# Two residual convolution layers on one core: statistics loads three chunks ahead, the next image's weights on GpSimd, and a reordered handover between the layers

## The chip, the cores and the metric

The kernel runs on one core of a Trainium2 chip. The metric is the device time of one execution in microseconds (us). It is given as the median of several executions, and one further execution was recorded by the profiler; the views quoted below come from that one.

## The reference, cut to what matters

The input `x` has four images of 64 channels and 256 x 256 pixels, in fp32. Two layers follow each other, and each adds its result to its input.

```python
# layer 0, on the group-normalized input
h  = gelu(conv3x3(gn(x), c1_w) + c1_b)
xa, k = split(conv1x1(h, c2_w), 2)
xs = gelu(conv_vertical3(conv_horizontal3(xa)))          # depthwise
w  = softmax(mean(xs) @ gate_w.T); keep the two largest of three
out = xs + sum_i w_i * w3_i @ ((w2_i @ k) * (w1_i @ xs))  # three low-rank experts
x = x + conv1x1(out, proj_w)
# layer 1, on the group-normalized result
h = relu(batchnorm(conv3x3(gn(x), quantized(w1))))        # statistics over all four images
h = batchnorm(conv3x3(h, quantized(w2)))                  # the same
x = x + relu(h + gn(x))
```

Both group norms need the mean and variance of a whole image before that image can be used, and both batch norms need those of all four images before anything behind them can start.

## The kernel before, in words

**Tiling.** The 128 partitions hold 64 channels of two image rows; an image has 128 such row pairs. A chunk is 8 row pairs (16 chunks an image, 1 MiB each), a group is 2, an octet is 4 (32 octets an image).

**Stages.** (1) The statistics of image 0 (`stats_load`, `stats_group`, `stats_end`, L370 to L416). (2) Layer 0 for four images, a software-pipelined loop of 32 steps an image, one octet a step. The 3x3 convolution is done as products over pixel pairs: GpSimd forms four sums and differences of neighbouring pixels in `v_ring` (`front_v`, L479), TensorE multiplies them with `c1s` and `u12` (`front_conv_a` and `_b`, through the helper at L436), ScalarE and VectorE undo the pair transform (`front_butterfly`, L545 to L547), ScalarE applies gelu (`front_h`, L553). Two and three steps later come the taps (`front_taps_a`, `_b`, `_h`, L602 to L620), the projection (`front_proj`, whose add on VectorE is L651), and the low-rank products (`front_k` L627, `front_q` L664 with L668 on VectorE). In the same loop, one image behind, `out_octets` adds the experts' part (L737 to L748), and one image ahead the next image's statistics are taken: `stats_load` issues one chunk on SyncE, `stats_group` is one `bn_stats` on VectorE (L383), and `stats_end` makes mean, scale and from these the next image's weights `c1s`, `u12` and the zero-point tile `v_edge` (L397 to L411). (3) `conv1`, the first convolution of layer 1, 32 blocks an image. Each chunk of the normalized image is split for it into an upper part (ScalarE, L343) and a lower part (the remainder; first cut of five rows on VectorE, second on GpSimd, L345), and so are sums of pixel pairs (GpSimd L353 and L361, ScalarE L359). A block is 16 products into `ps_h` and 4 into `ps_hm` (both L301), then ScalarE forms `m` (L324) and VectorE `h` (L325) and the batch statistics (L827). (4) `conv2` in the same manner. (5) The end: transfers, one ScalarE pass and two VectorE passes a chunk.

**What sets the order.** Everything from stage 2 on is written into a plan: `at(step, order, call)`, and within a step calls are issued by their order number. Each engine runs its own instructions in that order, and SyncE issues nearly all DMAs in that order too, so an instruction that waits holds up all behind it on its engine. In a step of layer 0 the orders that matter are: image loads 0, first products 1, outputs 2, statistics groups 3.5, taps 4, `divide` 5, projection 6, second products 7, butterfly 7.5, gelu 8.5, `front_v` 9 and 9.5, ps_k and ps_q 10, taps' exit 11, statistics load 11.5. The steps of conv1 use orders from 12 on. `divide` (L429) is a small memset on GpSimd (`tick`): it waits for the taps' last product, and the second products wait for it.

**The buffers concerned.** PSUM has two buffers of tag `c` (`ps_c`, `ps_h`), one of tag `a` (`ps_a`, `ps_hm`) and one of tag `p` (`ps_k`, `ps_p`, `ps_q`, `ps_o` and the small products of the statistics). SBUF tiles of tag `half` in `first_pool` hold statistics chunks (places called "s", two of them) and later the first pair of conv1's halves; work tiles "o" (three) hold statistics chunks of images 0 and 1 and later the outputs' chunks.

**The statistics' places and distance.** Images 0 and 1 use the places s, s, o, o, o in turn; images 2 and 3 the two s alone. In the plan, chunk k of image 1 is loaded three chunks ahead of its use, and chunks of images 2 and 3 one chunk ahead; 2.7 groups are taken a step:

```python
before, tags = (3, STATS_IN) if b == 1 else (1, STATS_IN[:2])
at(t + int((k - before) * CG / per), 11.5, stats_load, b, k, *tags[k % len(tags)])
```

**The handover.** Steps are counted on: image b begins at step 32 b, and `CONV1` is 128. The last image's steps from 128 on are spread out, three conv1 steps to one of layer 0 (`tail`, L873), so that octets 29 to 31 finish between conv1's first blocks. Of conv1's first image, chunks 0 to 3 have places of their own in the plan (`plan_conv1`), with the pixel-pair sums of a chunk made right after its split (`conv1_add_sums`).

Of the kernel before, what the change touches and what calls it, by code (L numbers as in the profile page):

```python
# [9 lines left out]
F32 = mybir.dt.float32  # L10
F32R = mybir.dt.float32r
# [51 lines left out]
def conv_preact_kernel(ctx: ExitStack, tc: tile.TileContext, io, col128, colset, col64):  # L63
# [51 lines left out]
    def half_pads(tiles):  # L115

        for t in tiles:
            nc.gpsimd.memset(t.bitcast(F32)[:, :, HW : HW + 1], 0.0)
        return tiles
# [2 lines left out]

        return t[:, a:e, :].rearrange("p a (e j) -> p a e j", e=2)[:, :, :, 0:HW]

    def sum_tiles(pool, name):
        return [pool.tile([P, CPAIR + 1, HW], F32R, tag="sum", name=f"sum_{name}{j}", bufs=4) for j in range(2)]

    def chunk_x(name):
        return first_pool.tile([P, CPAIR, PW], F32, tag="x", name=name, bufs=1)

    def split_tiles(pool, name):

        return [half_pads([half_tile(pool, f"half_{name}{i}{j}", 4) for j in range(2)]) for i in range(2)]


    lstat = layers.enter_context(tc.tile_pool(name="lstat", bufs=2))
# [196 lines left out]

    CUTS = (0, 5), (5, CPAIR + 1)

    def split(tiles, y, engines):

        parts = []
        for a, e in CUTS:
            upper, lower = (by_pixels(t, a, e) for t in tiles)  # L340
            parts.append((upper, lower, y[:, a:e, :].rearrange("p a (j e) -> p a e j", e=2)))
        for upper, _, y in parts:
            nc.scalar.activation(upper, y, AF.Copy)  # L343
        for (upper, lower, y), engine in zip(parts, engines):
            engine.tensor_tensor(lower, y, upper.bitcast(F32), ALU.subtract)  # L345
# [23 lines left out]

    def stats_load(b, k, tag, bufs):  # L370
        if tag == "s":
            t = flat(half_tile(first_pool, f"xs_in_{b}_{k}", 2, F32))[:, 0 : CPAIR * W]
            x_in[b, k] = t.rearrange("p (a b) -> p a b", b=W)
        else:
            x_in[b, k] = chunk_out(f"xs_in_{b}_{k}", tag, bufs)
        nc.sync.dma_start(flat(x_in[b, k]), x_s[b][:, k * CPAIR * W : (k + 1) * CPAIR * W])
# [8 lines left out]
    def stats_end(b):  # L385


        own = stat.tile([P, 2], F32, tag="gx", name=f"gx_{b}")
        yield from group_norm(st_x.pop(b), c128("avgx"), own, f"x{b}")
        yield  # L390
        gn1[b] = stat.tile([P, 2], F32, tag="gn1", name=f"gn1_{b}")
        v_edge[b] = lstat.tile([P, W // 2], F32, tag="v_edge", name=f"v_edge_{b}")
        ps = small(f"ps_gx_{b}")
        nc.tensor.matmul(ps[:, 0:2], c128("from_x"), own, start=True, stop=True)
        nc.vector.tensor_copy(gn1[b], ps[:, 0:2])
        c1s[b] = lstat.tile([P, 3, 3, C], F32, tag="c1s", name=f"c1s_{b}")
        nc.vector.tensor_scalar(  # L397
            c1s[b].rearrange("p a b c -> p (a b c)"), c128("c1"), gn1[b][:, 1:2], None, ALU.mult
        )
        nc.vector.tensor_scalar(v_edge[b], zeros[:, 0 : W // 2], gn1[b][:, 0:1], 2.0, ALU.add, ALU.mult)  # L400
        u12[b] = lstat.tile([P, 3, 2, C], F32, tag="u12", name=f"u12_{b}")
        ends = lstat.tile([P, 3, C], F32, tag="u_ends", name=f"u_ends_{b}", bufs=1)
        nc.vector.tensor_tensor(ends, c1s[b][:, :, 0, :], c1s[b][:, :, 2, :], ALU.add)
        for i, op in enumerate((ALU.add, ALU.subtract)):
            nc.vector.tensor_tensor(u12[b][:, :, i, :], ends, c1s[b][:, :, 1, :], op)

        nc.vector.tensor_tensor(ends[:, 0, :], u12[b][:, 0, 0, :], u12[b][:, 1, 0, :], ALU.add)
        for half in (slice(0, C), slice(C, P)):
            nc.vector.tensor_tensor(both[half, half], ends[half, 0, :], u12[b][half, 2, 0, :], ALU.add)
        u = u12[b].rearrange("p a b c -> p (a b c)")  # L410
        nc.vector.tensor_scalar(u, u, 0.5, None, ALU.mult)  # L411
# [394 lines left out]
    def conv1_b(b, d):  # L806
        k, i = d // 2, d % 2 * 2 * GP
        st = st_h[b]
        ps, ps_m = open_h.pop(b), bank("a", f"ps_hm_{b}_{d}")
        convolve_even(ps, "w1", halves[k % 2], i, 2 * GP)  # L810
        convolve_sum(ps_m, "w1", sums[k % 2], i, 2 * GP)
        if i == 0:

            if k % 2 and (b > 0 or k > 2):
                h_out[b] = chunk_x(f"h1_{b}_{k}").rearrange("p a b -> p (a b)")[:, 0 : CPAIR * W]
                h_out[b] = h_out[b].rearrange("p (a b) -> p a b", b=W)
            else:
# [25 lines left out]


    weights()
    STATS_IN = ("s", 2), ("s", 2), ("o", 3), ("o", 3), ("o", 3)
    for k in range(NCH):
        stats_load(0, k, *STATS_IN[k % 5])
        for g in range(k * CG, (k + 1) * CG):
            stats_group(0, g)  # L850
    for k in range(2):
# [20 lines left out]

    def tail(step):  # L873

        return step if step < CONV1 else CONV1 + 3 * (step - CONV1)

    def plan_front(b):
        t = b * F_STEPS
# [26 lines left out]
            at(place(t + 2 * j + 4), 10, front_k, b, j)  # L905
            at(place(t + 2 * j + 5), 10, front_q, b, j)
        e = place(t + NOCT + 3)
        at_each(((e, 2.5), (e, 5.7), (e, 8.7)) if e < CONV1 else ((e, 2.5), (e + 2, 12.7), (e + 4, 12.7)), gate(b))

    def plan_stats(b, t, per):  # L910

        for k in range(NCH):

            before, tags = (3, STATS_IN) if b == 1 else (1, STATS_IN[:2])
            at(t + int((k - before) * CG / per), 11.5, stats_load, b, k, *tags[k % len(tags)])
        for g in range(NG):
# [13 lines left out]

    conv1_pool, halves, sums = [], [], []

    def conv1_open():

        front.close()
        pool = layers.enter_context(tc.tile_pool(name="conv1", bufs=2, reuse_waits="tile"))
        conv1_pool.append(pool)
        halves.append(half_pads([half_tile(pool, f"half_11{j}", 2) for j in range(2)]))
        sums.extend(sum_tiles(pool, f"1{i}") for i in range(2))

    def plan_conv1(b):
# [75 lines left out]
        if k == NCH - 1:  # L1017
            nc.gpsimd.memset(h[0:C, CPAIR, :], 0.0)

    def conv2_split(i):  # L1020
        split(halves2[i % 2], h_in[i], (nc.vector, nc.vector))

    def conv2_add(i):
        sums_in[i] = add_pixels(h_in[i], f"2_{i}", halves_pool, "s", 2, [P, 5 * HW])
# [15 lines left out]
    sums2 = [sum_tiles(halves_pool, f"2{i}") for i in range(2)]  # L1040
    h2, st_h2 = {}, {}

    def chunk_h2(b, k):
# [27 lines left out]
    with tc.manual_schedule(  # L1071
# [179 lines left out]
```

## Time and profile before

| | |
|---|---|
| Median of 3 executions | 3432.7 us (3428.28 to 3432.73) |
| Profiled execution: its own time | 3435.02 us |
| Its span in the profile | 3433.2 us |
| Busy: TensorE, VectorE, ScalarE, GpSimd | 2753.0, 2723.4, 1673.7, 1593.8 us |
| 16 DMA engines | 838.28 MB, 73.3% of the span |
| Granted TensorE clock, mean | 0.91 |

The page shows the span in 40 equal slices, a digit for the busy tenths of each. Idle time of an engine costs nothing by itself; it costs where the engine is the one that all others wait for. So the views to read are those of waits: each line has who waited, for whom, how long in total, how often, and the longest. The timeline of one engine lists its instructions with start and length, and in brackets the idle time ahead of one and what ended it. In a plan like this one a wait is often put down to the neighbour in the queue and not to its cause: the instruction that the neighbour stands behind has to be looked up on its engine.

### The profile page before, as it was taken

To read this page: it belongs to the slowest core of one execution; us is meant where nothing else is said; L and a number is where in the kernel's file an instruction comes from. 1 tells how busy PE (TensorE), PEld (TensorE's weight loads), DVE (VectorE), ACT (ScalarE), POOL (GpSimd) and SP (SyncE) were. 2 spreads that over 40 slices of the span, in tenths; PEclk is the share of its full clock that TensorE was granted. 3 is DMA by queue.
4 is the path that set the end of the run, shared out by engine and by line. 5 is a ranking of instruction groups with operands and counts; after the bars stand their busy time and mean duration, and the time that the engine had idled before them with its cause. 6 is when DMAs were issued, how large, how long until landed. Compare 5 with 4: busy or idle time off the path is not lost.

```text
span 3433.2 us, 60883 instructions
## 1 busy us (share of the span) xinstructions
PE 2753.0 (80%) x24832; PEld 1764.3 (51%) x24832; DVE 2723.4 (79%) x2997; ACT 1673.7 (49%) x1831; POOL 1593.8 (46%) x1806
## 2 busy tenths in 40 slices
PE   2999999999999999996799999998999999400000
PEld 1555544454444545553577776786877777300000
DVE  7676578877878777774699999898999999856665
ACT  0444433343333344334466666676777777422222
POOL 2444433333333344443487878675777777200000
PEclk9999999999999999998899999999999999755555
DMA  8665578877887666774587888574666665599999
GB/s 301 171 186 119 149 220 256 242 207 223 236 257 229 202 190 203 217 208 140 174 286 271 304 283 285 205 261 167 239 235 240 235 232 183 177 412 413 412 412 384
DMA packets 365671, 838.28 MB, mean 244 GB/s; under 512 B 23312, under 2 KB 285968, under 8 KB 302672
## 3 DMA queue, kind: packets, MB, share of 16 engines
q1 hardware_dynamic: 365392, 834.40, 73.3%
q8 instruction: 195, 3.19, 0.4%
q14 instruction: 84, 0.69, 0.1%
HBM read 493.00 MB, written 341.31 MB: 243 GB/s over the span
## 4 chain that ended last, share of the span: by engine, by line
PE 70%; DMA 12%; DVE 10%; SPq 2%; ACT 2%; issue 2%; POOL 1%; ACTq 0%; DVEq 0%; POOLq 0%
PE ps_h L301 25%; PE ps_c L436 18%; DMA y_end<-y_d 9%; PE ps_a L436 8%; PE ps_k L627 4%; PE ps_h2m L301 3%; PE ps_o L737 3%; PE ps_p L436 3%; PE ps_hm L301 3%; PE ps_q L664 2%; DMA xs_in<-in_x 2%; DVE half L345 1%; DVE st_x L383 1%; DVE h L325 1%; SPq L1138 1%
## 5 line engine op out<-in xcount | busy, mean ns | idle before, releaser
L301 PE MATMUL ps_h<-half,w_q 128*128 128x512 f32 x4096 | 1033.0, 404 | 16.4 <-DVE h L325 10.3
L301 PEld LDWEIGHTS ps_h<-half,w_q 128*128 128x128 f32 x4096 | 778.6, 191 | 245.0 <-issue 29.6
L479 POOL TENSOR_TENSOR v_ring<-x 128x256 f32<-128x256 f32 x1024 | 596.8, 614 | 167.6 <-PE ps_c L436 119.0
L361 POOL TENSOR_TENSOR sum<-s,sum 128x640 fp32r<-128x640 f32 (+1 forms) x256 | 556.6, 2195 | 212.1 <-ACT sum L359 212.1
L436 PE MATMUL ps_a<-h,av 64*64 64x512 f32 (+1 forms) x3568 | 388.9, 537 | 22.3 <-ACT m L324 10.3
L325 DVE SCALAR_TENSOR_TENSOR h<-ps_h,scale_w,m 128x1024 f32<-128x1024 f32 x256 | 326.9, 1277 | 95.0 <-ACT m L324 95.0
L436 PE MATMUL ps_c<-v_ring,u 64*64 64x256 f32 (+1 forms) x6472 | 393.0, 374 | 8.3 <-POOL v_ring L479 4.8
L436 PE MATMUL ps_c<-v_ring,c1s 64*64 64x256 f32 (+1 forms) x6472 | 389.9, 371 | 4.6 <-POOL tick L429 4.2
L436 PEld LDWEIGHTS ps_c<-v_ring,u 64*64 64x64 f32 x6472 | 256.4, 135 | 244.3 <-issue 92.7
L429 POOL MEMSET tick<- 128x1 f32 x132 | 13.0, 99 | 758.2 <-PE ps_a L436 747.8
L436 PEld LDWEIGHTS ps_c<-v_ring,c1s 64*64 64x64 f32 x6472 | 263.4, 134 | 140.2 <-issue 45.6
L545 ACT ACTIVATE m<-ps_c 128x512 f32<-128x512 f32 x128 | 76.8, 600 | 493.6 <-PE ps_c L436 486.6
L620 ACT ACTIVATE xs<-t 128x1024 f32<-128x1024 f32 x128 | 135.5, 1059 | 320.7 <-DVE t L609 291.8
L1129 ACT ACTIVATE v<-y_end,shift,gn 128x2048 f32<-128x2048 f32 x64 | 134.0, 2096 | 321.9 <-DMA y_end<-y_d 315.1
L1130 DVE SCALAR_TENSOR_TENSOR h<-h,ss,v 128x2048 f32<-128x2048 f32 x64 | 150.2, 2351 | 161.3 <-ACT v L1129 115.6
L345 DVE TENSOR_TENSOR half<-h,half 128x1280 fp32r<-128x1280 f32 (+1 forms) x128 | 254.9, 2034 | 6.9 <-ACT half L343 6.9
L651 DVE TENSOR_TENSOR x<-ps_p,x 128x1024 f32<-128x1024 f32 x128 | 156.4, 1222 | 124.8 <-PE ps_p L436 110.6
L436 PEld LDWEIGHTS ps_a<-h,av 64*64 64x64 f32 x3568 | 165.9, 134 | 137.1 <-issue 82.5
L603 DVE SCALAR_TENSOR_TENSOR t<-ps_a,m,t 128x1020 f32<-128x1020 f32 x128 | 163.6, 1278 | 89.1 <-ACT t L602 88.9
L741 DVE SCALAR_TENSOR_TENSOR y<-ps_o,ob,y 128x512 f32<-128x512 f32 x256 | 189.5, 740 | 29.0 <-PE ps_o L737 28.2
L345 DVE TENSOR_TENSOR half<-yn,half 128x1280 fp32r<-128x1280 f32 x80 | 207.5, 2610 | 2.9 <-ACT half L343 2.9
L324 ACT ACTIVATE m<-ps_hm,m,scale_w 128x512 f32<-128x512 f32 x128 | 99.9, 780 | 218.8 <-PE ps_hm L301 218.8
(179 smaller groups left out, 4212.9 us busy)
## 6 DMA issues: line engine op xcount, KB each, us to landing
h_d<-h SPq DMA_DIRECT2D x117, 1024.0 KB, 4.8
h<-h_d SPq DMA_DIRECT2D x64, 1152.0 KB, 7.1
yn<-y_d SPq DMA_DIRECT2D x60, 1152.0 KB, 8.0
xs_in<-in_x SPq DMA_DIRECT2D x64, 1024.0 KB, 8.0
x<-in_x SPq DMA_DIRECT2D x256, 256.0 KB, 4.8
y<-t_d SPq DMA_DIRECT2D x64, 1024.0 KB, 7.8
y_d<-y SPq DMA_DIRECT2D x256, 256.0 KB, 4.4
y_end<-y_d SPq DMA_DIRECT2D x64, 1024.0 KB, 11.3
```

The lines of the kernel that those rows point to most:

```text
L301: nc.tensor.matmul(ps[:, 0 : n * HW], w[:, k, m, :], t[:, i + m : i + m + n, c : c + HW], start=(j == 0), stop=(j == len(terms) - 1),)
L325: nc.vector.scalar_tensor_tensor(h.rearrange("p a (b e) -> p e (a b)", e=2), by_two(ps)[:, :, 0 : n * HW], w_scale[w], m.unsqueeze(1).to_b ...
L345: engine.tensor_tensor(lower, y, upper.bitcast(F32), ALU.subtract)
L361: nc.gpsimd.tensor_tensor(tiles[1][:, a:e, :], t, tiles[0][:, a:e, :].bitcast(F32), ALU.subtract)
L436: last[:] = [nc.tensor.matmul(ps[o, at_out[0] : at_out[1], :], w[i], rhs[i], **flags)]
L479: nc.gpsimd.tensor_tensor(v_ring[:, o : o + 2, p, :], *terms[p])
L603: nc.vector.scalar_tensor_tensor(t[:, :, 1:W], ps[:, :, 0 : W - 1], sh[:, 0:1], t[:, :, 1:W], ALU.mult, ALU.add)
L620: nc.scalar.activation(flat(xss[b, n]), flat(t), AF.Gelu, accum_out=pooled[b][:, n : n + 1])
L627: nc.tensor.matmul(ps[32 * q : 32 * q + 32], wk[:, q % 2, t, :], flat(hs[b, 2 * j + q // 2, t]), start=(t == 0), stop=(t == 1),)
L651: nc.vector.tensor_tensor(t1, ps, t1, ALU.add)
L741: nc.vector.scalar_tensor_tensor(y, ps[:, 2 * n + g], out_bias[b], y, ALU.add, ALU.add)
L1130: nc.vector.scalar_tensor_tensor(h, h, ss2[:, 0:1], v, ALU.mult, ALU.add)
```

## The change

- Tag `half` in `first_pool` has four buffers instead of two. Images 0 and 1 take their statistics chunks in seven places (four s, three o), images 2 and 3 in the four s, and all loads in the loop are planned three chunks ahead.
- For images 1 to 3 the nine instructions that make `c1s`, `v_edge`, `u12` and `both` (L397 to L411) are issued on GpSimd instead of VectorE. In GpSimd's order they stand after the step's `v_ring` products and ahead of the next `tick`.
- The four buffers of tag `half` serve conv1 later: two for its first halves, two for its sums, which were tiles of their own in conv1's pool. So chunk 0's split and sums are both planned at the last step of layer 0 (127); chunk 1's split and sums move one step later but to order 5.5, right after `divide`.
- The tail of layer 0 is spread two steps apart instead of three, and the gate of the last image moves with it, to order 12.7.
- The first four blocks' `ps_hm` of image 0 use PSUM tag `c` instead of `a`.
- At the start of conv2 the first chunk's relu and split are issued cut by cut. The sums of conv2 take two buffers of tag `half` too (six in all).

As built, the order on each engine changes nowhere else. The two small memsets of the first halves land in GpSimd's order in image 2's loop.

```diff
-    def sum_tiles(pool, name):
-        return [pool.tile([P, CPAIR + 1, HW], F32R, tag="sum", name=f"sum_{name}{j}", bufs=4) for j in range(2)]
+    def sum_tiles(pool, name, bufs):
+
+        t = flat(half_tile(pool, f"sum_{name}", bufs))[:, 0 : 2 * (CPAIR + 1) * HW]
+        t = t.rearrange("p (u a b) -> p u a b", u=2, b=HW)
+        return [t[:, u] for u in range(2)]
...
-    def split(tiles, y, engines):
+    def split(tiles, y, engines, cuts=CUTS):
...
-            t = flat(half_tile(first_pool, f"xs_in_{b}_{k}", 2, F32))[:, 0 : CPAIR * W]
+            t = flat(half_tile(first_pool, f"xs_in_{b}_{k}", 4, F32))[:, 0 : CPAIR * W]
...
-        nc.vector.tensor_scalar(
+
+        engine = nc.gpsimd if b else nc.vector
+        engine.tensor_scalar(
             c1s[b].rearrange("p a b c -> p (a b c)"), c128("c1"), gn1[b][:, 1:2], None, ALU.mult
         )
...
-        ps, ps_m = open_h.pop(b), bank("a", f"ps_hm_{b}_{d}")
+        ps, ps_m = open_h.pop(b), bank("c" if b == 0 and d < 4 else "a", f"ps_hm_{b}_{d}")
...
-    STATS_IN = ("s", 2), ("s", 2), ("o", 3), ("o", 3), ("o", 3)
+    STATS_IN = (("s", 4),) * 4 + (("o", 3),) * 3
...
-        return step if step < CONV1 else CONV1 + 3 * (step - CONV1)
+        return step if step < CONV1 else CONV1 + 2 * (step - CONV1)
...
-        at_each(((e, 2.5), (e, 5.7), (e, 8.7)) if e < CONV1 else ((e, 2.5), (e + 2, 12.7), (e + 4, 12.7)), gate(b))
+        at_each(((e, 2.5), (e, 5.7), (e, 8.7)) if e < CONV1 else ((e + 1, 12.7), (e + 3, 12.7), (e + 5, 12.7)), gate(b))
...
-            before, tags = (3, STATS_IN) if b == 1 else (1, STATS_IN[:2])
+            before, tags = 3, STATS_IN if b == 1 else STATS_IN[:4]
...
+    def conv1_first():
+
+        halves.append(half_pads([half_tile(first_pool, f"half_10{j}", 4) for j in range(2)]))
+        sums.extend(sum_tiles(first_pool, f"1{i}", 4) for i in range(2))
+
     def conv1_open():
...
-        sums.extend(sum_tiles(pool, f"1{i}") for i in range(2))
...
-            at(t - 3, 0, lambda: halves.append(half_pads([half_tile(first_pool, f"half_10{j}", 2) for j in range(2)])))
+            at(t - 4, -1, conv1_first)
...
-                load, affine, ready = ((t - 4, t - 2, t - 1), (t - 1, t, t + 1), (t + 1, t + 3, t + 4), (t + 5, t + 7, t + 8))[k]
+                load, affine, ready = ((t - 4, t - 2, t - 1), (t - 1, t, t + 2), (t + 1, t + 3, t + 4), (t + 5, t + 7, t + 8))[k]
...
-            at(ready, 13.1, conv1_split, b, k)
+
+            at(ready, 5.5 if (b, k) == (0, 1) else 13.1, conv1_split, b, k)
             if b == 0 and k < 4:
-                at(max(ready, t), 13.2, conv1_add_sums, b, k)
+                at(ready, 5.6 if k == 1 else 13.2, conv1_add_sums, b, k)
...
         for cut in CUTS:
             conv2_affine(0, *cut)
+            conv2_split(0, (cut,))
         conv2_add(0)
-        conv2_split(0)
```

More of the change, by code (lines that the diff above doesn't have):

```diff
@@ L131, in split_tiles @@
     def split_tiles(pool, name):
-        return [half_pads([half_tile(pool, f"half_{name}{i}{j}", 4) for j in range(2)]) for i in range(2)]
+        return [half_pads([half_tile(pool, f"half_{name}{i}{j}", 6) for j in range(2)]) for i in range(2)]
     lstat = layers.enter_context(tc.tile_pool(name="lstat", bufs=2))
@@ L334, in conv_preact_kernel @@
     CUTS = (0, 5), (5, CPAIR + 1)
-    def split(tiles, y, engines):
+    def split(tiles, y, engines, cuts=CUTS):
         parts = []
-        for a, e in CUTS:
+        for a, e in cuts:
             upper, lower = (by_pixels(t, a, e) for t in tiles)
@@ L396, in stats_end @@
         c1s[b] = lstat.tile([P, 3, 3, C], F32, tag="c1s", name=f"c1s_{b}")
-        nc.vector.tensor_scalar(
+        engine = nc.gpsimd if b else nc.vector
+        engine.tensor_scalar(
             c1s[b].rearrange("p a b c -> p (a b c)"), c128("c1"), gn1[b][:, 1:2], None, ALU.mult
         )
-        nc.vector.tensor_scalar(v_edge[b], zeros[:, 0 : W // 2], gn1[b][:, 0:1], 2.0, ALU.add, ALU.mult)
+        engine.tensor_scalar(v_edge[b], zeros[:, 0 : W // 2], gn1[b][:, 0:1], 2.0, ALU.add, ALU.mult)
         u12[b] = lstat.tile([P, 3, 2, C], F32, tag="u12", name=f"u12_{b}")
         ends = lstat.tile([P, 3, C], F32, tag="u_ends", name=f"u_ends_{b}", bufs=1)
-        nc.vector.tensor_tensor(ends, c1s[b][:, :, 0, :], c1s[b][:, :, 2, :], ALU.add)
+        engine.tensor_tensor(ends, c1s[b][:, :, 0, :], c1s[b][:, :, 2, :], ALU.add)
         for i, op in enumerate((ALU.add, ALU.subtract)):
-            nc.vector.tensor_tensor(u12[b][:, :, i, :], ends, c1s[b][:, :, 1, :], op)
-        nc.vector.tensor_tensor(ends[:, 0, :], u12[b][:, 0, 0, :], u12[b][:, 1, 0, :], ALU.add)
+            engine.tensor_tensor(u12[b][:, :, i, :], ends, c1s[b][:, :, 1, :], op)
+        engine.tensor_tensor(ends[:, 0, :], u12[b][:, 0, 0, :], u12[b][:, 1, 0, :], ALU.add)
         for half in (slice(0, C), slice(C, P)):
-            nc.vector.tensor_tensor(both[half, half], ends[half, 0, :], u12[b][half, 2, 0, :], ALU.add)
+            engine.tensor_tensor(both[half, half], ends[half, 0, :], u12[b][half, 2, 0, :], ALU.add)
         u = u12[b].rearrange("p a b c -> p (a b c)")
-        nc.vector.tensor_scalar(u, u, 0.5, None, ALU.mult)
+        engine.tensor_scalar(u, u, 0.5, None, ALU.mult)
         yield
@@ L845, in conv_preact_kernel @@
     weights()
-    STATS_IN = ("s", 2), ("s", 2), ("o", 3), ("o", 3), ("o", 3)
+    STATS_IN = (("s", 4),) * 4 + (("o", 3),) * 3
     for k in range(NCH):
-        stats_load(0, k, *STATS_IN[k % 5])
+        stats_load(0, k, *STATS_IN[k % 7])
         for g in range(k * CG, (k + 1) * CG):
@@ L1018, in conv2_affine, with conv2_split @@
             nc.gpsimd.memset(h[0:C, CPAIR, :], 0.0)
-    def conv2_split(i):
-        split(halves2[i % 2], h_in[i], (nc.vector, nc.vector))
+    def conv2_split(i, cuts=CUTS):
+        split(halves2[i % 2], h_in[i], (nc.vector, nc.vector), cuts)
     def conv2_add(i):
@@ L1039, in conv_preact_kernel @@
     halves2 = split_tiles(halves_pool, "2")
-    sums2 = [sum_tiles(halves_pool, f"2{i}") for i in range(2)]
+    sums2 = [sum_tiles(halves_pool, f"2{i}", 6) for i in range(2)]
     h2, st_h2 = {}, {}
```

## The prediction, made before the changed kernel was run

> **What bounds the kernel now.** I read the page's slices first, then the waits of one image, then the timeline of each engine around the waits that the change touches. The slices (one is 85.8 us) show where TensorE isn't full:
>
> ```profile
> PE   2999999999999999996799999998999999400000
> PEclk9999999999999999998899999999999999755555
> DMA  8665578877887666774587888574666665599999
> ```
>
> TensorE is the bound from slice 2 to slice 34, but for slices 19 and 20, where layer 0 hands over to layer 1; the end is transfers alone and isn't touched. A 9 hides small gaps, so I summed layer 0's images (octet loop of 32 steps each) from one butterfly add of VectorE (L546) to that of the next image: images 0 to 3 take about 336, 395, 402 and 361 us. Image 3 has image 2's outputs beside it but no statistics. The waits of image 1, 430 to 800 us, name the difference (total, times, longest, in us):
>
> ```profile
> PE ps_k L627 <- DVE x L651: 16.0, 4, 4.4
> DVE st_x L383 <- DMA xs_in<-in_x: 15.5, 4, 4.9
> ```
>
> The timelines of SyncE, VectorE and TensorE around one of them (start, length, engine, instruction, idle before it and its releaser):
>
> ```profile
> 471.45 6.33 SPq L376 DMA_DIRECT2D xs_in<-in_x  x2
> ```
> ```profile
> 481.48 0.69 DVE L383 BATCH_NORM_STATS2 st_x<-xs_in 128x6 f32<-128x512 f32 x1 [4.07 <-DMA xs_in<-in_x]
> 482.09 1.21 DVE L651 TENSOR_TENSOR x<-ps_p,x 128x1024 f32<-128x1024 f32 x1
> ```
> ```profile
> 483.36 3.27 PE L627 MATMUL ps_k<-h,wk 128*32 128x512 f32 x16 [3.45 <-DVE x L651]
> ```
>
> The statistics load is issued at 471.5, VectorE needs it at 477.4, gets it at 481.5, and the add of the projection (L651) stands behind it in program order. That add frees the one PSUM buffer of tag p, for which TensorE's next product waits. It then runs slowly: 3.27 us, against 1.92 for the same sixteen at 754.07.
>
> The second place is the next image's weights, made on VectorE (L397 to L411):
>
> ```profile
> 739.58 0.91 DVE L397 TENSOR_SCALAR c1s<-m,gn 128x576 f32<-128x576 f32 x1
> ...
> 743.47 0.75 DVE L668 SCALAR_TENSOR_TENSOR low<-ps_q,m,k 128x512 f32<-128x512 f32 x1
> ```
> ```profile
> 744.27 1.13 PE L737 MATMUL ps_o<-ranks,wm 32*128 32x512 f32 x4 [1.71 <-DVE low L668]
> 745.33 3.55 PE L436 MATMUL ps_c<-v_ring,c1s 64*64 64x256 f32 x32
> ```
> ```profile
> 737.85 3.69 POOL L479 TENSOR_TENSOR v_ring<-x 128x256 f32<-128x256 f32 x6 [0.83 <-PE ps_c L436]
> 750.86 0.10 POOL L429 MEMSET tick<- 128x1 f32 x1 [9.33 <-PE ps_a L436]
> ```
>
> VectorE spends 3.9 us before low, which frees p; GpSimd is idle for 9.3 us meanwhile. The third place is the handover, TensorE's long waits:
>
> ```profile
> 1574.62 1.24 PE L436 MATMUL ps_c<-v_ring,c1s 64*64 64x256 f32 x11 [4.15 <-POOL tick L429]
> 1588.90 0.79 PE L301 MATMUL ps_hm<-sum,w_q 128*128 128x512 f32 x1 [4.86 <-ACT sum L359]
> 1606.13 1.98 PE L436 MATMUL ps_a<-h,av 64*64 64x512 f32 x8 [7.82 <-POOL tick L429]
> 1629.26 2.84 PE L436 MATMUL ps_a<-h,av 64*64 64x512 f32 x14 [10.27 <-ACT m L324]
> 1654.88 1.93 PE L664 MATMUL ps_q<-xs,m 128*32 128x512 f32 x8 [9.03 <-DVE x L651]
> 1684.59 2.08 PE L737 MATMUL ps_o<-ranks,wm 32*128 32x512 f32 x4 [6.30 <-issue]
> ```
>
> The fourth is the start of the second convolution:
>
> ```profile
> 2347.37 0.79 PE L301 MATMUL ps_h<-half,w_q 128*128 128x512 f32 x1 [5.23 <-ACT half L343]
> ```
>
> **What the Trainium skill says.** *TensorE: Matmul & The Clock Gate*, Part 1, the HAM clock gate: an idle window of about 3.4 us puts the array at half rate until a busy one has passed. The trace agrees in kind (3.27 against 1.92 after a wait of 3.45) and is stricter (3.55 against 1.96 after 1.71). So a wait costs its length and some 1 to 2 us more. *DMA: Bandwidth & Descriptors*, Rules for kernel authors: to overlap, issue a DMA early and wait on its semaphore late; here landing of these loads takes 8.0 us in the median, 17.3 at most. *GPSIMD Engine Reference*, 3.1 Elementwise: about 2.6 cycles an element at 1.2 GHz with two inputs, 1.03 with one; its section 8 says that it shares SBUF interfaces with VectorE. The trace agrees: L479's 256 elements take 614 ns, 2.4 ns each.
>
> **Part by part.** The sum is against the profiled execution: span 3433.2, 1.8 around it, 3435.0; that is 2.3 above the median of the runs shown, 3432.7.
>
> *Statistics of images 2 and 3 (in images 1 and 2's loop): loads three chunks ahead in four places.* One step is 11.0 us (with ps_q) or 11.8 (with ps_k), read between starts of L546 in steps without a wait. The steps from octet 1, 5, 6, 11, 12, 17 and 18 take 14.4, 15.3, 12.4, 16.3, 12.8, 16.3, 12.7 in image 1: over their rule by 3.4, 4.3, 0.6, 5.3, 1.0, 5.3, 0.9, in all 20.8. In image 2 they are over by 4.1, 6.8, 1.0, 5.2, 0.9, 4.7, 0.9: 23.6. Chunks 1, 4, 8 and 12 are those whose load stands at the end of an odd step, behind up to ten other issues, with its first use in the next step. Octet 2's step has a wait of 1.65 in image 1, worth about 0.75 in each image. In the new order each such load comes some 4.4 steps before its use, about 50 us against 17.3 at most: all waits go, 20.8 + 23.6 + 1.5 = **45.9**. What is late next is TensorE itself, as in the other steps. Place k+4 is freed by groups in the same step as its load or the one before, so SyncE can stand for part of a step; the image loads behind it are three steps ahead, so I cost that at nothing (if that cover went, see the third rival). Image 1's statistics keep their distance of three.
>
> *Seven places for the first image's statistics.* VectorE runs 61 of the groups back to back from 20.55 to 56.82, so earlier transfers help nothing there; the projection to GpSimd's first products (58.46) isn't on the path either, since TensorE starts at 67.99 after c1b. Nothing; bounds 0 and 1 gained.
>
> *Weights on GpSimd, images 1 to 3.* The steps from octet 27 take 14.9, 15.1 and 15.1 against 9.9, 11.0 and 11.0. About 0.65 of each is for the three small products between (ps_gx and its hand-over), which stay: 4.3 + 3.4 + 3.4 = **11.1** gained. GpSimd's nine instructions have no row; estimated with the page's 2.6 and 1.03 cycles, 768 elements with two inputs are 1.7 us, 1088 with one 0.9, and 0.3 fixed on the three tensor_scalars (L466: 0.33 for 16 elements) and little on six others: 3.8. The upper bound takes L361's contended 3.8 ns an element and twice the rest: 5.7. They start at 741.6 after the products of that step, and the next tick is due 4 us earlier than 750.9, near 747: a window of 5.4. So nothing, up to 1 lost in all; and no gain beyond, as nothing else shortens.
>
> *Handover.* I carried the new order on by hand from 1571.6, with each instruction at its duration of before. (1) The sums of chunk 0 now stand ahead of the ticks on GpSimd: 1.25 + 1.5 + 1.0 + 1.3 and two ScalarE steps of 0.7, so the tick comes at 1581.2, 6.6 later; the wait for sums goes, and the first block of conv1 ends 0.4 earlier (1591.8). (2) The add of octet 29 stands behind chunk 1's lower half, so ps_q waits 5.9; block 1 ends at 1607, 7 earlier. (3) With the sum products of blocks 0 to 3 in tag c, octet 31's taps no longer wait for m of block 2: at 1610 instead of 1629, and ps_k ends at 1620 instead of 1637. (4) But chunk 2's split now follows octet 31's gelu, m of block 2 follows its sums at 1637, and the last add follows that: ps_q waits some 14 us and ends at 1643 (1657 before), with block 3 at 1648. (5) Chunk 3's sums last until 1660, the gate's exp with its 1.3 us table load and the gate's 5 us on VectorE come before block 5's exit: the first ps_o of chunk 15 stands at 1683.4, against 1684.6. With 3 to 4 us for slow restarts after the longer waits, 2 us **lost**. Every handoff here is one of six in a row, so the bounds are 8 gained and 10 lost. DMAs: h1 and yn of chunk 5 move behind octet 31's stores, and are due 20 us later.
>
> *The second convolution's first halves.* The first block needs rows 0 to 4 alone, so its first half no longer waits for the second relu, 1.3 us; but the memset of row 0 (2345.04, 0.31) now ends just before: **0.6** gained (0 to 1.3). The sums come 0.9 later, covered by 16 products.
>
> Sum: 45.9 + 11.1 - 2 + 0.6 = 55.6 gained; 3435.0 - 55.6 = 3379.4, and 3377 on the median's scale; I say 3378.
>
> **The rivals.** *Half gain*: the lower TensorE rate has another cause than the waits, and other engines' waits fill the place. Then only TensorE's idle time goes, 27.4 us for statistics (16.0 and, in image 2's waits, 11.4) and 1.7 x 3 for weights, less 2: 3404.5, or 3402 on the median's scale. For it: rates differ between steps; against: undisturbed steps beside statistics take 11.0 and 11.8 just as in image 3. *A worse handover*: the longer waits at (1) and (4) add up, 12 lost in place of 2: 3388 (10 more than 3378). *SyncE stands* (slower): in images 1 and 2 each load of chunks 4 to 15 waits for a place that VectorE frees late, and image loads behind it miss their time. It decides once SyncE stands for over about 20 us of the 33 ahead; at 5 us for each of eight image loads in two images, 80 lost and the 46 not gained: 3432.7 - 9.7 + 80, about 3503. Against it: places come free within the step.
>
> **How the numbers follow.** Likeliest 0.68, with 3366 to 3388 from the handover's and the small bounds; half gain 0.14, worse handover 0.12, SyncE stands 0.04, and 0.02 that the statistics waits stay in another form and the handover eats the rest, near 3430. Under 0.2%, 7 us, a measurement can't tell a difference from none. Faster 0.94, same 0.02, slower 0.04. The range takes in the first three: 3364 to 3404.
>
> **What would show it.** Right: no statistics wait over 1 us in images 1 and 2; steps of 11.0 and 11.8 at octets 5, 11 and 17; images 1 and 2 near 370 and 375 us; nine instructions of about 4 us on GpSimd ending before a tick; ps_q of octets 30 and 31 waiting near 1641. Wrong: ps_k still waiting in those steps, image loads late, or the first tick of the handover after 1583 with later steps as late.

## The result, and the profile after

| | before | after |
|---|---|---|
| median of 4 runs each, same chip | 3432.26 | 3380.81 (3377.6 to 3382.82) |
| profiled execution | 3435.02 | 3380.32 |
| its span | 3433.2 | 3378.5 |

The ratio of the means is 0.9852, with an interval of 0.9835 to 0.9869 (every ratio below is one of means, against runs of the kernel before that were made beside it, with medians of 3431.2 to 3433.0). The gain is 51.5 us by the medians and 54.7 by the two profiled executions. The forecast was 3378, and 55.6 on the scale of the profiles. Below, 0.2% (7 us) is again what one comparison tells surely; smaller differences are read from the traces at fixed places, one trace a kernel, and how far such a reading wanders is said where it is used.

The slices of the changed kernel (one is 84.5 us) look like those of before. The gain lies inside the 9s:

```profile
PE   2999999999999999996899999998999999300000
PEclk9999999999999999997899999999999999755555
DMA  8675688878887767773688887664666664599999
```

So I read the lead instead: how much earlier than before a given instruction starts.

| place | lead, us |
|---|---|
| first butterfly add of image 0, 1, 2, 3 | 0.2, 3.6, 30.0, 54.9 |
| last butterfly add of image 3 | 55.0 |
| 14th exit of a conv1 block (VectorE's L328, which forms `h`, at 1674.65) | 52.9 |
| last exit of conv1 | 52.6 |
| first blocks of conv2 | 53.5 |
| span | 54.7 |

Images 1 and 2 now take 369.2 and 377.2 us (395.6 and 402.1 before); image 3, with the same statistics-free loop, takes 360.6 in both kernels. Of the 51.4 us by which the two images are shorter (7 of them from the weights), 33.1 were idle time of TensorE (45.3 before, 12.2 now). The other 18.3 are busy time: the same products take 734.1 us instead of 752.4. The clock shows why: in these two images of the kernel before, TensorE's granted clock was half in ten stretches of 3.4 or 6.8 us, 41.0 us in all. In the changed kernel there is none between 87 and 1520 us, which is all of layer 0 up to the handover.

These are VectorE's first waits in image 1 (430 to 770 us; total, times, longest), then TensorE's:

```profile
DVE t L608 <- ACT t L607: 17.0, 14, 1.4
DVE x L656 <- PE ps_p L441: 10.6, 10, 1.7
```
```profile
PE ps_p L441 <- DVE lg L690: 1.3, 1, 1.3
PE ps_o L742 <- DVE low L673: 1.0, 1, 1.0
```

VectorE's wait for `xs_in` (15.5 us before) is absent from the whole list, and so is TensorE's wait of 16.0 for the projection's add. The two that now come first on VectorE were there before (14.0 and 10.8). SyncE does stand for places, but briefly:

```profile
SPq L379 <- DVE st_x L386: 8.7, 4, 3.0
```

The weights, on GpSimd in image 1's last steps, and TensorE's product that used to wait 1.71 us there:

```profile
714.76 1.73 POOL L402 TENSOR_SCALAR c1s<-m,gn 128x576 f32<-128x576 f32 x1
...
719.94 1.17 POOL L416 TENSOR_SCALAR u<-u 128x384 f32<-128x384 f32 x1
721.05 0.10 POOL L434 MEMSET tick<- 128x1 f32 x1
```
```profile
715.94 1.13 PE L742 MATMUL ps_o<-ranks,wm 32*128 32x512 f32 x4
717.00 1.96 PE L441 MATMUL ps_c<-v_ring,c1s 64*64 64x256 f32 x32
```

The nine end 6.3 us after the first began and the tick stands directly behind the last: the cover is used up here, and not exceeded. The product waits for nothing, and the next 32 run at 1.96, not at 3.55.

The handover, TensorE's waits:

```profile
1525.94 1.54 PE L441 MATMUL ps_c<-v_ring,c1s 64*64 64x256 f32 x11 [10.40 <-POOL tick L434]
1546.16 1.93 PE L669 MATMUL ps_q<-xs,m 128*32 128x512 f32 x8 [5.63 <-DVE x L656]
1564.51 3.27 PE L632 MATMUL ps_k<-h,wk 128*32 128x512 f32 x16 [4.34 <-DVE x L656]
1589.04 1.94 PE L669 MATMUL ps_q<-xs,m 128*32 128x512 f32 x8 [13.75 <-DVE x L656]
1610.86 2.08 PE L304 MATMUL ps_hm<-sum,w_q 128*128 128x512 f32 x4 [4.57 <-ACT m L327]
1626.12 1.87 PE L742 MATMUL ps_o<-ranks,wm 32*128 32x512 f32 x4 [4.19 <-DVE y L746]
```

These are other waits than before, but as long in sum: the lead shrinks from 54.96 to 52.94 here. The wait of 13.75 becomes plain on ScalarE:

```profile
1580.43 0.74 ACT L362 ACTIVATE sum<-s 128x640 fp32r<-128x640 f32 x1 [3.98 <-POOL s L356]
1583.93 0.63 ACT L362 ACTIVATE sum<-s 128x512 fp32r<-128x512 f32 x1 [2.76 <-POOL s L356]
1584.46 0.76 ACT L327 ACTIVATE m<-ps_hm,m,scale_w 128x512 f32<-128x512 f32 x1
```

`m` of block 2 stands in ScalarE's order behind the two copies of chunk 2's sums, and these wait for GpSimd. Behind `m` come the block's exit on VectorE (1585.26), then the last projection's add (1587.78), which frees tag p for ps_q. Chunk 2's sums themselves aren't needed by anything in that chain. In the kernel before they stood ahead of the same `m` too (copies at 1624.53 and 1627.91, `m` at 1628.44): octet 31's taps waited 10.27 us for it there.

The start of the second convolution, with 4.66 where 5.23 stood:

```profile
2294.23 0.80 PE L304 MATMUL ps_h<-half,w_q 128*128 128x512 f32 x1 [4.66 <-ACT half L346]
```

### The profile page after: what moved, and what is told of

Read it like the earlier page. It is cut to its first block, busy times and chain, and to the rows that moved or that the text cites. A ratio compares the mean times of both kernels' runs of the same rounds, so it can differ in the third digit from the quotient of the medians.

```text
span 3378.5 us, 60896 instructions
## 1 busy us (share of the span) xinstructions
PE 2732.3 (81%) x24832; PEld 1756.3 (52%) x24832; DVE 2701.3 (80%) x2970; ACT 1670.7 (49%) x1831; POOL 1611.0 (48%) x1833
## 4 chain that ended last, share of the span: by engine, by line
PE 69%; DMA 12%; DVE 10%; ACT 3%; issue 3%; SPq 2%; POOL 2%; ACTq 0%; POOLq 0%; DVEq 0%
PE ps_h L304 24%; PE ps_c L441 19%; DMA y_end<-y_d 10%; PE ps_a L441 9%; PE ps_k L632 3%; PE ps_h2m L304 3%; PE ps_o L742 3%; PE ps_p L441 3%; PE ps_hm L304 2%; PE ps_q L669 2%; DMA yn<-y_d 1%; DVE h L328 1%; DVE st_x L386 1%; DVE half L348 1%; SPq L1148 1%
## 5 line engine op out<-in xcount | busy, mean ns | idle before, releaser
L484 POOL TENSOR_TENSOR v_ring<-x 128x256 f32<-128x256 f32 x1024 | 597.1, 616 | 158.7 <-PE ps_c L441 112.0
L364 POOL TENSOR_TENSOR sum<-s,sum 128x640 fp32r<-128x640 f32 (+1 forms) x256 | 556.1, 2192 | 200.1 <-ACT sum L362 194.4
L328 DVE SCALAR_TENSOR_TENSOR h<-ps_h,scale_w,m 128x1024 f32<-128x1024 f32 x256 | 327.0, 1277 | 101.3 <-ACT m L327 96.7
L441 PE MATMUL ps_c<-v_ring,c1s 64*64 64x256 f32 (+1 forms) x6472 | 387.7, 369 | 10.8 <-POOL tick L434 10.4
L434 POOL MEMSET tick<- 128x1 f32 x132 | 13.1, 99 | 690.5 <-PE ps_a L441 679.7
L348 DVE TENSOR_TENSOR half<-h,half 128x1280 fp32r<-128x1280 f32 (+1 forms) x128 | 254.5, 2029 | 7.7 <-ACT half L346 7.7
L348 DVE TENSOR_TENSOR half<-yn,half 128x1280 fp32r<-128x1280 f32 x80 | 196.7, 2475 | 5.1 <-ACT half L346 5.1
```

What stands on the lines that cost most here:

```text
L328: nc.vector.scalar_tensor_tensor(h.rearrange("p a (b e) -> p e (a b)", e=2), by_two(ps)[:, :, 0 : n * HW], w_scale[w], m.unsqueeze(1).to_b ...
L364: nc.gpsimd.tensor_tensor(tiles[1][:, a:e, :], t, tiles[0][:, a:e, :].bitcast(F32), ALU.subtract)
L441: last[:] = [nc.tensor.matmul(ps[o, at_out[0] : at_out[1], :], w[i], rhs[i], **flags)]
L484: nc.gpsimd.tensor_tensor(v_ring[:, o : o + 2, p, :], *terms[p])
```

## The experiments

All start from the changed kernel, undo or move a part of it, and leave nothing out. "Handover" below is the lead at conv1's 14th exit less the lead at image 3's last butterfly add, both against the kernel before: what the stage itself gains. It is -2.0 in the changed kernel. Five traces have the same code in the handover (the changed kernel and experiments 1, 2 and 5) and give -1.6 to -3.2, so a single reading is good to about 1 us either way. A "stand" is an instruction held up behind others in its engine's order.

**1. Distance one, and distance two.** My theory was that the loads' distance makes the gain; the rivals were that the two more places do it, or that half of it isn't in the waits. The second kernel has 2 for the 1.

```diff
-            before, tags = 3, STATS_IN if b == 1 else STATS_IN[:4]
+            before, tags = (3, STATS_IN) if b == 1 else (1, STATS_IN[:4])
```

> The changed kernel with the loads of images 2 and 3 planned one chunk ahead again; the four places and all else stay. If the distance is what the change gained most by, each load that stands at the end of an odd step is late again: VectorE waits some 32 us in images 1 and 2, their steps from octets 1, 5, 11 and 17 go back to 14 to 17 us, and the time rises by 44 (images 1 and 2 got 26.5 and 24.8 us shorter, less 3.5 each for the weights) to about 3425. The rival, that the lower TensorE rate had another cause than these waits, expects only TensorE's idle time of 27 us, about 3408, with ps_k still at 1.9 us after a wait. A third theory, that four places and not the distance did it, expects no change, 3381.

> The changed kernel with those loads two chunks ahead. A chunk is 1.5 steps or some 17 us, so two chunks leave about 2.9 steps or 33 us for a landing of 8.4 us in the median plus the issues ahead of it. If only being late costs, this is as good as three: no VectorE wait on a statistics chunk, 3381 within 4. If SyncE's queue or crowded DMA engines eat the distance, some waits of 1 to 5 us come back: 3385 to 3400.

Measured: one chunk ahead 3428.64 (ratio 0.9991, 0.9982 to 1.0000), two chunks ahead 3381.49 (0.9851, 0.9837 to 0.9866). With distance one the waits are back, as VectorE and TensorE show for image 1 (430 to 800 us):

```profile
DVE st_x L386 <- DMA xs_in<-in_x: 14.4, 3, 5.0
```
```profile
PE ps_k L632 <- DVE x L656: 12.8, 3, 4.5
```

Distance one costs 47.8 us although the four places are there (the account had 44). Images 1 and 2 take 394.5 and 396.7 us with it; without the 3.5 that the weights give in each, that is 398.0 and 400.2, against 395.6 and 402.1 in the kernel before. So the places alone give nothing. Two chunks ahead are as good as three.

**2. Weights back on VectorE.**

```diff
-        engine = nc.gpsimd if b else nc.vector
+        engine = nc.vector
```

> The changed kernel with the nine weight instructions of images 1 to 3 back on VectorE. My account, from the steps from octet 27 (14.9, 15.1, 15.1 before; 11.5, 11.6, 11.7 after), expects 10 us more, about 3391, with a TensorE wait of 1.7 us behind low and products at half rate after it in each image. The rival, that the loads already took the pressure off VectorE so that these 4 us now hide, expects 3381 to 3384.

Measured: 3390.66 (0.9878, 0.9863 to 0.9893), 9.9 slower. The product waits again:

```profile
721.21 1.13 PE L742 MATMUL ps_o<-ranks,wm 32*128 32x512 f32 x4 [1.71 <-DVE low L673]
```

**3. The handover undone**: last steps three apart, gate, `ps_hm` in tag a, chunk 1's affine, split and sums at their old orders and chunk 0's sums one step later, as before. The places of the sums stay.

```diff
-        return step if step < CONV1 else CONV1 + 2 * (step - CONV1)
+        return step if step < CONV1 else CONV1 + 3 * (step - CONV1)
...
-            at(ready, 5.5 if (b, k) == (0, 1) else 13.1, conv1_split, b, k)
+            at(ready, 13.1, conv1_split, b, k)
...
-                at(ready, 5.6 if k == 1 else 13.2, conv1_add_sums, b, k)
+                at(max(ready, t), 13.2, conv1_add_sums, b, k)
...
```

> The changed kernel with the old handover: tail three steps apart, the gate's old places, the sums of chunk 0 after the ticks and chunk 1's split at its old step, ps_hm of the first blocks in tag a. Sums stay in the buffers of tag half. My account expects the new handover to have lost 2 us (the traces' offset falls from 55.0 at octet 31's butterfly to 52.9 in the steady part of conv1), so this one comes to about 3379, a difference that only the traces can tell; the first tick 6.5 us earlier, octet 31's taps again behind m of block 2. The rival, that the new handover gained, expects 3385 to 3391.

Measured: 3375.64 (0.9835, 0.9820 to 0.9850), 5.2 less than the changed kernel. The two intervals overlap, so the traces have to tell. The handover is +1.1 instead of -2.0. The profiled execution is 7.1 us shorter than the changed kernel's: 3.1 are this, and 2.9 a start that happened to be earlier by the end of image 0's first two steps. Experiment 4 has the old handover as well and gives +0.9, while the new one gives -1.6 to -3.2: the new order is worse than the old one, by some 3 us.

**4. The loads and their places alone**: the third kernel, with the weights on VectorE and conv2's start in its old order besides.

```diff
-        engine = nc.gpsimd if b else nc.vector
+        engine = nc.vector
...
-            conv2_split(0, (cut,))
         conv2_add(0)
+        conv2_split(0)
```

> The loads alone: seven and four places and three chunks ahead, with the weights on VectorE, the old handover (as in the run with the handover undone, 3375.6) and conv2's first halves in the old order; the sums stay in buffers of tag half. If the parts add up, this is 3431 less 46 for the loads, and 1 to 2 for the handover's sums being allocated elsewhere: 3383 to 3387. If the loads need the weights' move to pay (VectorE relieved), it is above 3390.

Measured: 3389.16 (0.9881, 0.9861 to 0.9900), 43.9 under its own runs of before, 3433.02. It fell between the two expectations. In its trace images 1 and 2 take 371.4 and 379.3 us: 24.2 and 22.7 less, 47.0 in all, of which 1.3 and 1.2 are in the step with the weights (13.8 and 13.9 instead of 15.1). So about a third of what the weights cost in those images went with the late loads; why isn't shown. This run also shows what conv2's new order gives: from the end of conv1 to the first product of conv2 its lead doesn't grow (43.2 at both), while that of the changed kernel grows by 0.6 (52.57 to 53.14).

**5. More places for image 0.** Five places instead of seven for the first images' statistics.

```diff
-    STATS_IN = (("s", 4),) * 4 + (("o", 3),) * 3
+    STATS_IN = (("s", 4),) * 2 + (("o", 3),) * 3
...
```

> The changed kernel with the statistics of images 0 and 1 in five places again (two s, three o); images 2 and 3 keep their four. My account gives nothing to the two more places, since VectorE runs image 0's groups back to back: 3381 within 3, and VectorE's last group of image 0 at 56.8 us as in both kernels. If the first transfers were a limit, it is 3 to 10 us slower.

Measured: 3380.45 (0.9861, 0.9842 to 0.9881), no change.

**6. The sum products of the first blocks back in tag a.**

```diff
-        ps, ps_m = open_h.pop(b), bank("c" if b == 0 and d < 4 else "a", f"ps_hm_{b}_{d}")
+        ps, ps_m = open_h.pop(b), bank("a", f"ps_hm_{b}_{d}")
```

> The changed kernel with ps_hm of the first four blocks in tag a again, so that octet 30's and 31's taps wait until m of blocks 0 and 1 is read. In the changed kernel those m come some 3 and 2 us after the taps could start, so my account expects 2 to 6 us lost in the handover, 3382 to 3387. If the second buffer of tag c was worth more to ps_h than tag a to the taps, it gains: 3375 to 3380.

Measured: 3379.93 (0.9860, 0.9837 to 0.9884), no change by the medians; the handover is -3.9, 0.7 to 2.3 us worse than the five with tag c, where I expected 2 to 6. The profile shows why it isn't more:

```profile
1559.79 2.84 PE L441 MATMUL ps_a<-h,av 64*64 64x512 f32 x14 [2.19 <-ACT m L327]
...
1589.06 1.94 PE L669 MATMUL ps_q<-xs,m 128*32 128x512 f32 x8 [13.75 <-DVE x L656]
```

Octet 31's taps do wait again, and start at 1559.79 instead of 1556.51. But the wait of 13.75 isn't reached by way of tag a, and swallows it: ps_q starts at 1589.06, against 1589.04 in the changed kernel.

**7. The sums of chunks 0 to 3 later.** If ScalarE's and GpSimd's in-order queues make the handover's waits, sums that aren't needed yet should move behind the work that is. Chunk 0's sums go behind the tick, chunk 1's split behind the exit of octet 30's taps (order 11.5), its sums behind the tick of step 132, two steps on, and the sums of chunks 2 and 3 behind the exits of blocks 2 and 4.

```diff
+            if b == 0 and k < 4:
+                at(ready, 11.5 if k == 1 else 13.1, conv1_split, b, k)
+                at(*((t, 8.6), (t + 4, 5.1), (t + 5, 13.05), (t + 9, 13.05))[k], conv1_add_sums, b, k)
-            at(ready, 5.5 if (b, k) == (0, 1) else 13.1, conv1_split, b, k)
-            if b == 0 and k < 4:
-                at(ready, 5.6 if k == 1 else 13.2, conv1_add_sums, b, k)
             else:
+                at(ready, 13.1, conv1_split, b, k)
```

> The changed kernel with the sums of conv1's first four chunks planned elsewhere, their work unchanged: chunk 0's after the ticks and octet 31's gelu (step 128, order 8.6), chunk 1's split behind octet 30's taps (130, 11.5) and its sums behind the tick of step 132 (132, 5.1), chunks 2 and 3's sums behind m of block 2 and 4 (13.05 of steps 133 and 137). My account of the handover says that its waits are places in the queues of ScalarE and GpSimd: carried on by hand, the first tick comes 6.5 us earlier, ps_q of octet 30 no longer waits for chunk 1's half, the last ps_q ends near 1570 instead of 1591, and conv1 goes on 15 to 20 us earlier, near 3363. The rival, that the handover is bound by the amount of work on ScalarE and GpSimd or by the loads of chunks 4 and 5, expects 3376 to 3381.

Measured: **3352.03** (0.9780, 0.9759 to 0.9802), 28.8 less than the changed kernel by the medians, 24.7 by the ratios; the account had 15 to 20. It is the fastest of all kernels here. Its handover is +23.7 instead of -2.0. So I took it apart: chunk 0's sums alone, chunk 1's split and sums alone, the sums of chunks 2 and 3 alone.

> The changed kernel with the sums of layer 1's chunk 0 alone put after octet 30's tick on GpSimd. Theory: the handover is a chain in which every stand counts, so the 24 us that moving all four chunks' sums brought there are made of parts; the first wait for the tick falls from 10.4 to 3.8 us, and that alone gives 5 to 7: near 3375. Rival: only the last stand counts (ps_q waits 13.8 us for the add that stands behind chunk 2's sums), and it takes the 6.6 back: 3379 to 3382.

> The changed kernel with chunk 1's split and sums alone put later (the split behind the step's last affine, the sums in the step after the tick). Theory: ps_q's wait of 5.6 us falls by 1 to 3, and GpSimd's products leave the block before octet 31's tick: 2 to 6 gained, near 3377. Rival: the sums now stand ahead of chunk 2's halves on GpSimd and lengthen the wait of 13.8: 3380 to 3386. The three parts should come near the 29 of all four if they are a chain, well over or under it if one stand covers another.

> The changed kernel with the sums of chunks 2 and 3 alone put later. Theory: the longest wait (13.8 us of ps_q) goes to about 5.6 us and the ps_hm wait of 4.6 goes, so 10 to 14 us: near 3369. Rival: the add of the last projection waits for octet 31's gelu and chunk 2's halves in any case, so it gives under 3: 3378 to 3382; or this is nearly all of the 29: 3353 to 3360.

| moved | median | ratio, interval | handover | over the changed kernel's |
|---|---|---|---|---|
| nothing | 3380.81 | 0.9852 (0.9835 to 0.9869) | -2.0 | |
| chunk 0's sums | 3377.74 | 0.9841 (0.9827 to 0.9854) | +3.5 | 5.5 |
| chunk 1's split and sums | 3378.45 | 0.9840 (0.9826 to 0.9853) | +1.7 | 3.7 |
| sums of chunks 2 and 3 | 3364.17 | 0.9803 (0.9789 to 0.9816) | +13.1 | 15.1 |
| all | 3352.03 | 0.9780 (0.9759 to 0.9802) | +23.7 | 25.7 |

The parts add up to 24.4 of 25.7: a chain, with no stand that covers another. Expected were 5 to 7, 2 to 6 and 10 to 14; the rivals, that only the last stand counts or that it counts for nearly nothing, don't fit. (By the ratios the parts add up to 24.7 of 24.7; by medians they are 3.1, 2.4 and 16.6, in all 22.1 of 28.8. Within conv1 the changed kernel's lead wanders between 50.7 and 55.7, so the fixed place is the better scale.) With chunk 0's sums moved, the tick's wait falls from 10.40 to

```profile
1519.41 1.33 PE L441 MATMUL ps_c<-v_ring,c1s 64*64 64x256 f32 x11 [3.81 <-POOL tick L434]
```

With those of chunks 2 and 3 moved, `m` passes the copies on ScalarE, and ps_q gets its buffer 8.4 us earlier:

```profile
1576.07 0.77 ACT L327 ACTIVATE m<-ps_hm,m,scale_w 128x512 f32<-128x512 f32 x1
1580.18 0.74 ACT L362 ACTIVATE sum<-s 128x640 fp32r<-128x640 f32 x1 [3.34 <-POOL s L356]
```
```profile
1580.66 1.93 PE L669 MATMUL ps_q<-xs,m 128*32 128x512 f32 x8 [5.63 <-DVE x L656]
```

**8. The last steps three apart**, all else as changed: is it the distance that lost what the third experiment gave back?

```diff
-        return step if step < CONV1 else CONV1 + 2 * (step - CONV1)
+        return step if step < CONV1 else CONV1 + 3 * (step - CONV1)
```

> The changed kernel with layer 0's last steps three blocks of conv1 apart again, and the rest of its handover kept. Theory: the distance isn't what lost the 5.2 us that undoing the whole handover gave back; with the other places laid for two apart, three apart is no better: 3380 to 3386. Rival: the distance is the loss (less work to hide each handoff), and three apart gives 5 or more back: 3376 or less.

Measured: 3380.82 (0.9851, 0.9838 to 0.9865), to 0.01 us the changed kernel's median; handover -0.8, which is 0.8 to 2.4 better than the five traces of the new order. So the distance can be a part of the 3 us that the new order loses, but not all of it; tag c loses nothing (experiment 6). Left are the places of chunk 0's sums, of chunk 1's affine, split and sums, and of the gate. Experiment 7 shows that the sums of the first two cost 5.5 and 3.7 where they now stand, but which of these lost against the old order isn't shown one by one. The sums of chunks 2 and 3 stand ahead of `m` in both orders.

## Why the prediction was right, step by step

**The loads: right.** Predicted 45.9, measured 44.4 in the changed kernel (images 1 and 2 are 26.4 and 24.9 shorter, less 3.5 each in the step with the weights). At the steps listed in the working, image 1 gave 21.7 (predicted 20.8), image 2 only 20.6 (predicted 23.6); octet 2's step gave 1.1 and 1.0 (0.75 each). Image 2's steps from octets 5 and 6 still take 12.3 and 12.5, not 11.0 and 11.8: there the rule read from other steps was too low. Image 3, which has no statistics at all, takes 11.9 and 12.5 at these two, so the rule could have been read there. Another 0.7 is missing at octet 18 of image 2 (12.3; 11.6 with distance two): the memset of the first halves stands on GpSimd there, waits 6.95 us for a statistics group, and the tick is behind it (993.64). The 4.4 steps that each load now has are more than it needs, since two chunks ahead do as well. (Image 0's 336 us in the working counts from TensorE's first product; from its first butterfly add it is 329.5. Nothing rests on it.)

**The half-gain rival: refuted.** It allowed 27.4 for the statistics, which is TensorE's idle time alone; 44.4 came. TensorE's busy time fell as well, by 18.3 us in images 1 and 2 for the same products, and with distance one it is back (374.2 and 373.9 us against 364.6 and 369.5, at a clock of 0.97 and 0.98 against 1.00). So the slow products belong to the waits, as the 3.27 against 1.92 had said; the granted clock was 0.58 in those 3.27 us and 0.53 in the 3.55 behind the wait of 1.71. The Trainium skill's clock-gate section (*TensorE: Matmul & The Clock Gate*, Part 1) has the same kind of effect behind a longer idle window than this case's 1.71.

**SyncE stands: refuted.** It stands 8.7 us for these places in image 1 (11.6 in the kernel before) and 7.3 in image 2, in four waits each of at most 3.6, and from image 1 to image 3 no compute engine waits for an image load; the rival needed over 20.

**The weights: right, one term mis-sized.** Predicted 11.1; by the lead, 3.4, 3.5 and 3.5, in all 10.3; by taking it back, 9.9. GpSimd's nine instructions take 6.3 us, not 3.8, and more than the upper bound of 5.7. The one-input products are the greater part of the error: 1.73 us for 576 elements and 1.17 for 384, both 3.0 ns an element, where the estimate from *GPSIMD Engine Reference*, 3.1, had 0.86 ns. (The page gives 1.03 cycles for a loop of at most two operations an element and doesn't name this instruction; the working took it for that.) The six two-input ones take 2.8 us, not 1.7. The measurement decides. The cost is about 1 us, in image 0, whose step from octet 27 takes 11.5 instead of about 10.5, with a wait of TensorE for the tick of 0.79; in images 1 and 2 the tick comes just behind the ninth and nothing waits.

**The handover: the sum right, one reason wrong.** Predicted 2 lost, measured 2.0. With 55 added, the first tick stands at 1580.9 (predicted 1581.2), ps_q waits 5.63 (5.9), the last ps_q 13.75 (some 14) and stands at 1644.0 (its end was put at 1643). But step (3) gave tag c the credit for octet 31's taps, 1629 down to 1610 (1611.5 measured). Experiment 6 takes tag c away, and they move by 3.3 alone; the rest of the 17.8 is the new order. The stands were carried forward to within some 3.5 us: block 1 ends at 1609.5 (1607), block 3 at 1651.5 (1648), and ps_o of chunk 15 comes at 1681.1 (1683.4). That the sum came out to the microsecond is in part luck. And the new order was taken as given: of no stand was it asked whether what stood in front was needed. That was 26 us.

**Seven places and the second convolution: right.** No change with five places; at conv2's start the lead grows by 0.6 up to the first product (predicted 0.6), and not at all where the old order is kept (experiment 4).

In the sum of the profiles: 0.2 at the start, 44.4, 10.3, -2.0, -0.4 in conv1, +0.9 over the first blocks of conv2 and +1.3 to the end give the measured 54.7. The terms of conv1 and the end weren't forecast; whether they are more than the wandering of the lead stays open, as does why the lead wanders.

## What to carry to other kernels

A load whose wait sits in front of an in-order queue costs more than its wait, since what is behind it stalls another engine that then restarts slowly; one more chunk of distance paid, a third paid nothing, so try distances one by one. When work is spread over engines that run in order, list for each long wait what stands in front of the releasing instruction on its engine, and ask whether that is needed by then: here sums that nobody waited for stood in front of `m` and of the tick, and moving them gave 25 to 29 us, about half of what the whole change gave. Judge the edits of such a stage one at a time at a fixed place in the trace, and read from kernels that share its code how far that reading wanders, for a change that is right in sum can carry a part that loses.

## What the runs showed of the hardware that was not expected

On GpSimd a one-input product with a per-partition scalar is not cheaper than a two-input operation: 3.0 ns an element (576 in 1.73 us) against 2.4 for L484's two-input operations of 256 elements (0.61 us) and 3.1 for L408's of 192 (0.59 us). The three of each in the trace take 1.73 to 1.74 and 1.17 us, and the second took that with VectorE busy for half of it as for most of it.

And one and the same GpSimd operation varies with what VectorE does beside it. The three 1024-element adds below are the same line:

```profile
1516.43 2.68 POOL L348 TENSOR_TENSOR half<-yn,half 128x1024 fp32r<-128x1024 f32 x1 [11.89 <-ACT half L346]
...
1543.23 4.01 POOL L348 TENSOR_TENSOR half<-yn,half 128x1024 fp32r<-128x1024 f32 x1 [4.14 <-ACT half L346]
...
1616.17 2.42 POOL L348 TENSOR_TENSOR half<-yn,half 128x1024 fp32r<-128x1024 f32 x1 [0.84 <-ACT half L346]
```

It isn't how busy VectorE is: it was busy in 1.5 us of the first and 2.9 of the second, but in 2.4 of the third too, and in 98% of the time of the fourteen such adds that take 2.40 to 2.47. What differs is VectorE's own part of the split (L348, 1280 elements, both inputs in SBUF). It lies beside the second for all of its 1.47 us, beside the first for 0.42, and beside those fourteen not at all. Elsewhere it is VectorE's that gives way: beside the GpSimd add at 1599.66, which keeps its 2.43, it takes 3.60. Where the two lie wholly beside each other, the slowed one thus takes about as long as both (2.4 and 1.5) one after the other. The small subtraction L364 shows the same: 640 elements take 1.53 to 1.57 us in the seven with no L348 of VectorE beside them, and 2.43 to 2.88 in all 101 that have one beside them for over 1.2 us. That fits section 8 of the *GPSIMD Engine Reference* (SBUF interfaces shared with VectorE, in contention when VectorE's instruction has two inputs in SBUF), but no run here varied it on purpose, and what decides which of the two gives way stays open.
